# Row gathers of a graph layer with a routed feed-forward: issued in two runs, or paced by GpSimd copies

## The chip, the core and the metric

The kernel runs on one core of a Trainium2 chip. The core has a matrix engine (TensorE, PE in the profile, with its weight loads as PEld), a vector engine (VectorE, DVE), an activation engine (ScalarE, ACT), a general engine (GpSimd, POOL) and a queue engine that only issues transfers (SyncE, SP). Each engine works through its own list of instructions in order and waits on semaphores where it needs another engine's result. Transfers between the main memory and the on-chip buffers are moved by 16 DMA engines. The metric is the time of one execution on the device in microseconds (us). Three plain executions of the kernel before took 451.36 to 452.05 us, with a median of 451.93 us.

## The reference, cut to what matters

`x` has 6250 rows of 256 numbers (nodes), `src` and `dst` name the two ends of 100000 edges. The first layer is a graph attention, of which only the first 6250 edges are used:

```python
xt = jnp.matmul(x, weight).reshape(-1, heads, out_ch)       # x is layer-normed
row, col = (edge_index[0], edge_index[1])                   # src, dst
alpha_l = einsum('ehd,hd->eh', xt[row], attn_l)
alpha_r = einsum('ehd,hd->eh', xt[col], attn_r)
alpha = softmax(leaky_relu(alpha_l + alpha_r, 0.01), axis=1)
tmp = einsum('nh,nhd->nd', alpha[:n], xt[col[:n]])
out = broadcast_to(tmp[:, None, :], (n, heads, out_ch))
```

The second layer is a mixture of 8 experts with the two best of each row. A router multiplies each normed row with 8 vectors, the two largest probabilities are kept and scaled to one, and the row gets the weighted sum of two feed-forward results:

```python
logits = tokens @ router_w.T
rw, re = top_k(softmax(logits), 2); rw = rw / rw.sum(-1)
for e in range(8):
    y = gelu(tokens @ w1[e] + b1[e]) @ w2[e] + b2[e]
    out = out + combine[:, e:e+1] * y
```

Both layers add their input to their result.

## The kernel before, in words

The 6250 rows are cut into 49 tiles of 128 (`NT`), each row of a tile on one partition. The tiles form five groups, `GROUPS`, of 9, 12, 12, 9 and 7. The order of the work on each engine is the order in which the program names it; nothing is moved by a planner.

**Loads.** SP loads `x` in pieces of four tiles into one buffer for each group (`xs`), then a broadcast of the source indices (`highs` to `high_1`, L348 and L349). The row `x[dst]` that a tile needs is fetched by GpSimd: `gather(t)` (L232) is one indirect transfer of 128 rows of 1 KB. The 49 gathers land in a buffer of 9 tiles (`xd_own`) and in one of 31 tiles (`big`); tiles 40 to 48 use the places of tiles 0 to 8 again, so their gathers wait until those tiles are used up. The experts' second weights and biases are later loaded into `big` too.

**Own terms.** The first loop runs over 13 blocks of up to four tiles (`OWN`). For each block, `turn` transposes the tiles of `x` on PE (L243) and ACT copies them out (L247). `own_terms(k)` multiplies them with 12 columns on PE (L417), and ACT copies the result to the buffer `own_T` (L421), of which there are two, kept under the tag `pxs`. `back(k)` turns that result back (L430), one block later. Beside it DVE takes the statistics of the rows (`source_statistics`), and small jobs named in `fillers` are put behind blocks 1, 2, 7 and 8. The last pass of the loop turns the first block of gathered rows.

**Features.** The second loop runs over the 49 tiles in blocks of up to four. `features(g, i, ...)` multiplies the turned gathered tile with 293 columns on PE (L463), ACT copies the result to `pxs` (L471) and takes the sum of squares of the gathered row (L473, written to `junk`). `look_up` finds the attention term of the source row by matrix products (L492, L496) that DVE reduces (L500). Behind the last tile of a group, `feature_root(g)` computes the reciprocal root on GpSimd (L454 and L455). The attention and routing of group g are worked during group g+1, spread over its tiles by `tasks`: `attend_1` (from L507 on DVE), `exponents` (L521 on ACT), `attend_2`, `attend_3` (L539, L544, L545) and `route`, which ends with the write of the group's rows to a table (L588 on SP).

**After the loops.** The last group's attention and routing run alone; the rows are sorted by their pair of experts, the table's rows are gathered in that order (L897 on GpSimd), and 125 units of two matrix products each (L1073 and L1089) run the experts.

**The gathers' order.** GpSimd first makes one small copy, `last_x` (L634), that reads a late piece of `x`; so no gather starts before that piece has landed. Then come 37 gathers without anything between them. The other 12 come in `last_gathers`, which is called behind `feature_root(0)`, that is after tile 8 of the second loop; behind `feature_root(1)` `counting` makes two index tables with GpSimd (L702, L706).

Of the kernel before, what the change touches and what calls it, by code (L numbers as in the profile page):

```python
# [9 lines left out]
FP = mybir.dt.float32  # L10
# [12 lines left out]
def kernel(  # L23
# [36 lines left out]
    nc = tc.nc  # L60
# [3 lines left out]
    P = 128  # L64
    NT = -(-N // P)
    LAST = N - (NT - 1) * P
    GROUPS = [(0, 9), (9, 12), (21, 12), (33, 9), (42, 7)]
# [37 lines left out]
    held = early.enter_context(tc.tile_pool(name="held", bufs=1))  # L105
# [26 lines left out]
    xs = [held.tile([P, n, R], FP, name=f"x{g}") for g, (_, n) in enumerate(GROUPS)]  # L132
# [29 lines left out]
    def xd(t):  # L162
        k, of = (t - NOWN, big) if NOWN <= t < NOWN + BIG else (t % (NOWN + BIG), xd_own)
        return of[:, k * D : (k + 1) * D]
# [8 lines left out]
    def tiny(name, n, bufs=2):  # L173
        return small.tile([P, n], FP, name=name, bufs=bufs, tag=name)
# [33 lines left out]
    for of, pattern, k in ((count_up, [[1, 128]], 0), (number, [[0, 1]], 1)):  # L208
        nc.gpsimd.iota(
            of, pattern=pattern, base=0, channel_multiplier=k,  # L210
# [20 lines left out]
    def gather(t):  # L231
        nc.gpsimd.indirect_dma_start(  # L232
            out=xd(t), out_offset=None, in_=x[:, :],
            in_offset=bass.IndirectOffsetOnAxis(ap=dst_sb[:, t : t + 1], axis=0),
        )

    def turn(of, t0, n):

        blocks = []
        for c in range(DC):  # L240
            pt = ps.tile([128, n * P], FP, name="pt", tag="t")
            for i in range(n):
                nc.tensor.transpose(  # L243
                    pt[:, i * P : (i + 1) * P], of(t0 + i)[:, c * 128 : (c + 1) * 128], ident
                )
            tT = work.tile([128, n * P], FP, name="tT", bufs=4)
            nc.scalar.copy(tT, pt)  # L247
            blocks.append(tT)
        return blocks
# [3 lines left out]
    OWN = [  # L253
        (q, t0 + k, min(4, n - k)) for q, (t0, n) in enumerate(PARTS) for k in range(0, n, 4)
    ]
# [152 lines left out]
    rstds, own_Ts, pas = {}, {}, {}  # L408
    def source_statistics(q):
        t0, n = PARTS[q]  # L410
        rstds[q] = statistics(x_of, t0, n)

    def own_terms(k, blocks):
        n = OWN[k][2]
        pa = ps.tile([H + NE, n * P], FP, name="pa1", tag="m")
        for c in range(DC):
            nc.tensor.matmul(  # L417
                pa, own[:, c, :], blocks[c], start=(c == 0), stop=(c == DC - 1)
            )
        own_T = work.tile([H + NE, n * P], FP, name="own_T", tag="pxs")  # L420
        nc.scalar.copy(own_T, pa)  # L421
        own_Ts[k] = own_T

    def back(k):
        q, t0, n = OWN[k]
        if t0 == PARTS[q][0]:
            pas[q] = ps.tile([P, PARTS[q][1], H + NE], FP, name="pa2", tag="r")
        own_T = own_Ts.pop(k)
        for i in range(n):
            nc.tensor.transpose(  # L430
                pas[q][:, t0 - PARTS[q][0] + i, :], own_T[:, i * P : (i + 1) * P],
                ident[: H + NE, : H + NE],
            )

    def source_end(q):
        t0, n = PARTS[q]
        std = tiny("std", n)
        nc.scalar.activation(std, rstds.pop(q)[:, :, 1], AF.Sqrt, bias=eps_c)
        rstd = tiny("rstd", n)
        nc.vector.reciprocal(rstd, std)  # L440
        pa, at = pas.pop(q), slice(t0, t0 + n)
        rest = small.tile([P, H, n], FP, name="al_f")
        nc.vector.tensor_tensor(
            rest.rearrange("p h t -> p t h"), pa[:, :, :H], wide(rstd, H), ALU.mult
        )
        for k in range(3):
            nc.vector.tensor_copy(al_sb[:, k, :, at], rest)
            if k < 2:
                nc.vector.tensor_tensor(rest, rest, al_sb[:, k, :, at], ALU.subtract)
        nc.vector.tensor_copy(own_r[:, at, :], pa[:, :, H:])  # L450
# [6 lines left out]
    pxss, sqs, rstd_ds = {}, {}, {}  # L457

    def features(g, i, blocks, k):

        px = ps.tile([P, C], FP, name="px", tag="px")
        for c in range(DC):
            nc.tensor.matmul(  # L463
                px, blocks[c][:, k * P : (k + 1) * P], w_sb[:, c, :],
                start=(c == 0), stop=(c == DC - 1),
            )
        if i == 0:
            pxss[g] = work.tile([P, GROUPS[g][1], C], FP, name="pxs")
            sqs[g] = tiny("sq", GROUPS[g][1], 3)
        pxs = pxss[g]  # L470
        nc.scalar.copy(pxs[:, i, :], px)  # L471
        junk = work.tile([P, D], FP, name="junk", bufs=1)
        nc.scalar.activation(  # L473
            junk, xd(GROUPS[g][0] + i), AF.Square, bias=pxs[:, i, MEAN:],
            accum_out=sqs[g][:, i : i + 1],
        )

    def feature_root(g):
        rstd_ds[g] = tiny("rstd_d", GROUPS[g][1], 3)
        root(rstd_ds[g], sqs.pop(g), 1.0 / D)  # L480
# [149 lines left out]

    last_x = held.tile([P, 1], FP, name="last_x")
    nc.gpsimd.tensor_copy(last_x, xs[3][:, 7, :1])  # L634
    FIRST = 37
    for t in range(FIRST):
        gather(t)
    fillers = {
        1: weights_columns,
        2: pair_tables,  # L640
# [11 lines left out]
    def turn_features(k):  # L652
        g, b, n = FEATURES[k]
        return turn(xd, GROUPS[g][0] + b, n)

    source_statistics(0)
    for k, (q, t0, n) in enumerate(OWN):
        after = turn(x_of, *OWN[k + 1][1:]) if k + 1 < len(OWN) else turn_features(0)
        own_terms(k, blocks)
        blocks = after  # L660
        if k > 0:
            back(k - 1)
        if k == 0 or OWN[k - 1][0] != q:
            if q > 0:
                source_end(q - 1)
            if q + 1 < len(PARTS):
                source_statistics(q + 1)
        if k in fillers:
            fillers[k]()
# [23 lines left out]
    CUT = 26  # L693
    steps_b = mid.tile([P, TS, CUT], BF, name="steps_b", bufs=1)
    count_b = mid.tile([P, NTE], BF, name="count_b", bufs=1)
    def last_gathers():

        for t in range(FIRST, NT):
            gather(t)

    def counting():
        nc.gpsimd.iota(  # L702
            steps_b, pattern=[[1, TS], [0, CUT]], base=0, channel_multiplier=0,
            allow_small_or_imprecise_dtypes=True,
        )
        nc.gpsimd.iota(  # L706
            count_b, pattern=[[1, NTE]], base=0, channel_multiplier=0,
            allow_small_or_imprecise_dtypes=True,
        )
# [4 lines left out]
    def settle():  # L714
        while pending:
            pending.pop(0)()

    def tasks(g):

        n = GROUPS[g][1]  # L720
        at = {i: [] for i in range(n)}

        def put(i, what):
            at[min(i, n - 1)].append(what)

        if g >= 1:
            f = g - 1
            m = GROUPS[f][1]
            put(1, lambda: attend_1(f))
            put(2, lambda: exponents(f))  # L730
            put(2, lambda: attend_2(f))
            for i in range(0, m, 3):
                put(3 + i // 3, lambda i=i: attend_3(f, i, min(3, m - i)))
            steps = route(f)
            for i in range(5):
                put(7 + i // 2, lambda: next(steps))
        if g >= 2:
            f2 = g - 2
            put(1, lambda: rank(f2))
            put(2, lambda: ranked(f2))  # L740
        if g == 3:
            put(0, load_experts)
        if g == 4:
            put(0, load_biases)
        return at

    at = {}
    for k, (g, b, n) in enumerate(FEATURES):
        if b == 0:
            at = tasks(g)  # L750
        after = None
        for j in range(n):
            i = b + j
            features(g, i, blocks, j)
            if j == 0 and k + 1 < len(FEATURES):
                after = turn_features(k + 1)
            settle()
            if i % 2:
                pending.append(look_up(g, i - 1, 2))
            elif i == GROUPS[g][1] - 1:  # L760
                pending.append(look_up(g, i, 1))
            if i == GROUPS[g][1] - 1:
                feature_root(g)
                if g < 2:
                    (last_gathers, counting)[g]()
            for what in at[i]:
                what()
        blocks = after
# [4 lines left out]
    n = GROUPS[z][1]  # L773
# [73 lines left out]
    for t0, t1 in ((0, CUT), (CUT, NTE)):  # L847
        at, n = slice(t0, t1), t1 - t0
# [266 lines left out]
    for u in range(NU + LAG):  # L1115
# [17 lines left out]
        k, step = divmod(u, 4)  # L1133
# [46 lines left out]
```

## Time and profile before

The profile is of one execution that was recorded instruction by instruction. It has its own time, which differs from that of the plain executions:

| what | value |
|---|---|
| median of three plain executions | 451.93 us (451.36 to 452.05) |
| the recorded execution | 496.15 us |
| its span, first to last instruction | 494.4 us |
| mean granted clock of TensorE | 0.896 |
| PE busy | 391.3 us (79%) |
| DVE busy | 311.3 us (63%) |
| ACT busy | 227.7 us (46%) |
| POOL busy | 197.3 us (40%) |
| gathers of rows, L232 | 49, of 0.94 us each in the median, 23.7 to 129.3 us |
| expert stage, first L1073 to the end | about 250 to 494 us |

The page of a profile gives each engine's busy time, a strip of the span in 40 slices of 12.4 us, the chain of work that ended last, and the costliest groups of instructions. Behind the page, one can ask for the busy time of each engine in chosen stretches, for the instructions of one engine in order of time with what they waited for, and for the chain in order of time. An idle time whose releaser is "issue" is one in which the engine waited for nothing that the profile shows; "remote" and "another core or an unknown queue" name a releaser that is not among this core's recorded instructions.

### The profile page before, as it was taken

The page shows a single profiled execution, that of the slowest core. Times are in us where ns is not written, and L with a number is a line of the kernel's source. Part 1 is how long each engine was busy: PE and PEld are TensorE (multiplying, and loading weights), DVE is VectorE, ACT ScalarE, POOL GpSimd, SP SyncE. Part 2 cuts the span into 40 slices and gives each one's busy share as a digit, 9 for nine tenths or more (in the row PEclk, how much of TensorE's full clock was granted, in tenths as well). Part 3 has the DMA queues.
Part 4 walks back from the last instruction along what each step waited for, and adds up shares of the span by engine and source line. Part 5 has one row for each costly group of instructions (what it writes and reads, how often), then busy time and mean ns, then how long its engine had stood idle before and what let it go on. Part 6 is the DMA issues. An engine that isn't in the chain of part 4 may idle for free.

```text
span 494.4 us, 9535 instructions
## 1 busy us (share of the span) xinstructions
PE 391.3 (79%) x2442; PEld 321.8 (65%) x2442; DVE 311.3 (63%) x1051; ACT 227.7 (46%) x656; POOL 197.3 (40%) x241
## 2 busy tenths in 40 slices
PE   6970308998999971035699999999999999999992
PEld 4430003576787751024579999888988888999991
DVE  4911327425567879884368788777877687655562
ACT  2440004576676652000456675657565656633330
POOL 0177750008452101002553544676666563423232
PEclk9996557999899996555699999999999999999997
DMA  7989540003503864302666666767666676566631
GB/s 239 306 190 128 115 92 1 1 0 77 181 0 117 222 194 173 111 0 65 195 180 195 187 179 186 217 204 216 207 202 204 194 204 186 177 195 183 193 92 30
DMA packets 59091, 74.61 MB, mean 151 GB/s; under 512 B 7154, under 2 KB 54086, under 8 KB 58784
## 3 DMA queue, kind: packets, MB, share of 16 engines
q1 hardware_dynamic: 51488, 52.45, 35.1%
q0 software_dynamic: 7248, 21.29, 16.7%
q8 instruction: 22, 0.36, 0.3%
q10 hardware_dynamic: 304, 0.27, 0.2%
q14 instruction: 29, 0.24, 0.2%
HBM read 59.13 MB, written 14.87 MB: 150 GB/s over the span
## 4 chain that ended last, share of the span: by engine, by line
PE 64%; DVE 13%; issue 10%; ACT 6%; POOL 2%; another core or an unknown queue 2%; ACTq 1%; DMA 1%; POOLq 0%
PE ph L1073 21%; PE py L1089 18%; PE px L463 6%; PE pa L417 4%; PE pt L243 4%; DVE pxs L539 3%; PE pt L1019 2%; PE pi L862 2%; DVE pxs L544 2%; PE pl L492 1%; POOL xr L897 1%; ACT hid L1080 1%; DVE x L545 1%; ACT tok L986 1%
## 5 line engine op out<-in xcount | busy, mean ns | idle before, releaser
L1073 PEld LDWEIGHTS ph<-tokT,w 128*128 128x128 f32 x1000 | 131.1, 194 | 21.3 <-ACT tokT L1020 13.1
L1073 PE MATMUL ph<-tokT,w 128*128 (+1 forms) x1000 | 136.3, 280 | 7.1 <-ACT tokT L1020 6.5
L1089 PE MATMUL py<-big,hid 128*128 x500 | 129.5, 382 | 0.1
L1080 ACT ACTIVATE hid<-ph,b_cols 128x128 f32<-128x128 f32 x250 | 78.3, 366 | 99.2 <-PE ph L1073 70.0
L1089 PEld LDWEIGHTS py<-big,hid 128*128 128x128 f32 x500 | 86.0, 192 | 7.3 <-DVE acc L1096 0.4
L1096 DVE SCALAR_TENSOR_TENSOR acc<-py,shares,acc 128x256 f32 (+1 forms) x125 | 60.5, 484 | 37.9 <-PE py L1089 15.7
L1100 POOL DMA_INDIRECT out_dram<-acc,held_by x49 | 53.0, 1081 | 74.8 <-DVE acc L1096 60.6
L897 POOL DMA_INDIRECT xr<-table,held_by x49 | 49.5, 1010 | 56.4 <-DVE held_by L884 40.0
L1096 DVE SCALAR_TENSOR_TENSOR acc<-big,shares,acc (+1 forms) x125 | 60.7, 486 | 8.9 <-issue 4.9
L463 PE MATMUL px<-w_sb,tT 128*128 128x293 f32 x196 | 56.8, 422 | 3.1 <-ACT pxs L471 2.7
L986 ACT ACTIVATE tok<-xr,nm 128x256 f32<-128x256 f32 x49 | 29.7, 605 | 46.9 <-DVE xr L993 39.0
L247 ACT COPY tT<-pt 128x512 f32<-128x512 f32 (+2 forms) x54 | 27.2, 541 | 42.5 <-issue 18.5
L463 PEld LDWEIGHTS px<-w_sb,tT 128*128 128x128 f32 x196 | 34.8, 193 | 10.9 <-ACT pxs L471 3.2
L243 PE MATMUL pt<-ident,x 128*128 128x128 f32 x98 | 17.5, 329 | 28.1 <-ACT tT L247 21.5
L454 POOL TENSOR_SCALAR sq<-sq 128x9 f32<-128x9 f32 (+2 forms) x5 | 1.2, 245 | 83.8 <-ACT junk L473 70.6
L232 POOL DMA_INDIRECT big<-in_x_dram,dst_sb x31 | 29.4, 949 | 10.2 <-issue 9.2
L243 PEld LDWEIGHTS pt<-ident,x 128*128 128x128 f32 x98 | 13.3, 168 | 30.8 <-ACT tT L247 21.9
L471 ACT COPY pxs<-px 128x293 f32<-128x293 f32 x49 | 19.7, 403 | 25.5 <-PE px L463 21.3
L1008 ACT ACTIVATE acc<-xr,nm 128x256 f32<-128x256 f32 x49 | 29.2, 598 | 0.0
L417 PE MATMUL pa<-tT,own 128*12 128x512 f32 (+1 forms) x52 | 26.5, 637 | 0.0
L1019 PE MATMUL pt<-ident,tok 128*128 128x128 f32 x98 | 19.3, 280 | 7.8 <-ACT tok L986 7.8
L500 DVE TENSOR_REDUCE ag<-pl 128x8 f32<-128x392 f32 (+1 forms) x26 | 13.9, 538 | 14.9 <-PE pl L496 14.9
(206 smaller groups left out, 484.9 us busy)
## 6 DMA issues: line engine op xcount, KB each, us to landing
w<-in_L_ffn_w_dram SPq DMA_DIRECT2D x125, 256.0 KB
x<-in_x_dram SPq DMA_DIRECT2D x11, 512.0 KB
table<-x SPq DMA_DIRECT2D x2, 2022.0 KB
table<-x SPq DMA_DIRECT2D x2, 1516.5 KB
big<-in_L_ffn_w_dram SPq DMA_DIRECT2D x2, 1024.0 KB
high<-highs SPq DMA_DIRECT2D x1, 1568.0 KB
table<-x SPq DMA_DIRECT2D x1, 1179.5 KB
big<-in_L_ffn_b_dram SPq DMA_DIRECT2D x1, 1024.0 KB
```

What stands on the lines that cost most here:

```text
L232: nc.gpsimd.indirect_dma_start(out=xd(t), out_offset=None, in_=x[:, :], in_offset=bass.IndirectOffsetOnAxis(ap=dst_sb[:, t : t + 1], axis=0),)
L243: nc.tensor.transpose(pt[:, i * P : (i + 1) * P], of(t0 + i)[:, c * 128 : (c + 1) * 128], ident)
L417: nc.tensor.matmul(pa, own[:, c, :], blocks[c], start=(c == 0), stop=(c == DC - 1))
L463: nc.tensor.matmul(px, blocks[c][:, k * P : (k + 1) * P], w_sb[:, c, :], start=(c == 0), stop=(c == DC - 1),)
L897: nc.gpsimd.indirect_dma_start(out=xr[:, i, :], out_offset=None, in_=table[:, :], in_offset=bass.IndirectOffsetOnAxis(ap=held_by[:, s0 + i ...
L986: nc.scalar.activation(tok[:, i, :], xr[:, i, :D], AF.Identity, bias=bias[:, i : i + 1], scale=scale[:, i : i + 1],)
L1008: nc.scalar.activation(acc[:, s * D : (s + 1) * D], xr[:, i, :D], AF.Identity, bias=bias[:, i : i + 1], scale=more[:, i : i + 1],)
L1073: nc.tensor.matmul(ph[:, j, :], w[:, c * F + j * 128 : c * F + (j + 1) * 128], tokT[:, bass.ds(rows_at + c * TS, TS)], start=(c == 0), sto ...
L1080: nc.scalar.activation(hid[:, j, :], ph[:, j, :], AF.Gelu, bias=b1_cols[:, :, j][:, bass.ds(at_act[u][0], 1)])
L1089: nc.tensor.matmul(py, hid[:, j, :], we2[:, j, bass.ds(at_pe[u][1], D)], start=(j == 0), stop=(j == FC - 1),)
L1096: nc.vector.scalar_tensor_tensor(to, y, share, to, op0=ALU.mult, op1=ALU.add)
L1100: nc.gpsimd.indirect_dma_start(out=ends_at[s][:, :], out_offset=bass.IndirectOffsetOnAxis(ap=held_by[:n, s : s + 1], axis=0), in_=acc[:n, ...
```

## The change

The copy `last_x` and the run of 37 gathers behind it are taken out, and so is `last_gathers` with its 12. A helper, `paced(t, n, of)`, makes one small GpSimd copy that reads `of`, so that GpSimd waits until `of` is written, and then issues the gathers of tiles t to t+n-1. It is called in two places. In the loop over own terms it comes behind each of the last ten blocks (k = 3 to 12), reads that block's `own_T` (12 partitions, one element each) and issues two gathers, 20 in all. In the loop over features it comes behind each tile's `features`, reads one column of that tile's `pxs` (128 partitions, one element each) and issues the gather of the tile 20 further on; this happens for tiles 0 to 28, 29 gathers. `counting` stays behind `feature_root(1)`.

```diff
-    last_x = held.tile([P, 1], FP, name="last_x")
-    nc.gpsimd.tensor_copy(last_x, xs[3][:, 7, :1])
-    FIRST = 37
-    for t in range(FIRST):
-        gather(t)
+    AHEAD = 20
+    OWN_FROM = len(OWN) - AHEAD // 2
+    pace = held.tile([P, 1], FP, name="pace")
+
+    def paced(t, n, of):
+
+        nc.gpsimd.tensor_copy(pace[: of.shape[0]], of)
+        for i in range(t, min(t + n, NT)):
+            gather(i)
+
...
         own_terms(k, blocks)
+        if k >= OWN_FROM:
+            paced(2 * (k - OWN_FROM), 2, own_Ts[k][:, :1])
         blocks = after
...
-    def last_gathers():
-
-        for t in range(FIRST, NT):
-            gather(t)
-
...
             features(g, i, blocks, j)
+            if GROUPS[g][0] + i + AHEAD < NT:
+                paced(GROUPS[g][0] + i + AHEAD, 1, pxss[g][:, i, :1])
...
                 feature_root(g)
-                if g < 2:
-                    (last_gathers, counting)[g]()
+                if g == 1:
+                    counting()
```

## The prediction

> **What bounds the kernel now.** I read the page's strip first and found a hole in an otherwise busy PE row at about 36 to 76 us. Then I asked for the busy times by stretch there. Columns: stretch, its length, busy us (and instructions) of PE, PEld, DVE, ACT, POOL, then the granted clock, the DMA share and GB/s.
>
> ```profile
> 24.00:36.00 12.00, 10.02 (x49) 4.38 (x48) 1.37 (x55) 5.00 (x9) 9.26 (x10) 1.00 0.81 191
> 36.00:48.00 12.00, 0.41 (x4) 0.32 (x4) 1.36 (x13) 0.67 (x2) 8.41 (x10) 0.66 0.94 115
> 48.00:60.00 12.00, 4.95 (x12) 1.83 (x12) 1.94 (x10) 0.96 (x2) 8.96 (x11) 0.50 0.53 126
> 60.00:72.00 12.00, 1.24 (x5) 0.50 (x4) 4.91 (x15) 0.57 (x1) 8.22 (x9) 0.64 0.48 104
> 72.00:84.00 12.00, 7.47 (x27) 3.44 (x28) 7.19 (x35) 4.55 (x9) 0.00 (x0) 0.63 0.03 6
> 84.00:96.00 12.00, 11.94 (x65) 5.64 (x63) 6.50 (x21) 6.45 (x15) 0.00 (x0) 1.00 0.00 1
> ```
>
> For 36 us PE and ACT nearly stand still while POOL issues gathers (0.94 us each, one per 1.25 us). ACT's list in order of time says who holds whom:
>
> ```profile
> 35.89 0.57 ACT L421 COPY own_T<-pa 12x512 f32<-12x512 f32 x1 [2.97 <-PE pa L417]
> 47.79 0.58 ACT L247 COPY tT<-pt 128x512 f32<-128x512 f32 x1 [11.33 <-issue]
> 55.52 0.58 ACT L247 COPY tT<-pt 128x512 f32<-128x512 f32 x1 [7.14 <-issue]
> 66.72 0.57 ACT L421 COPY own_T<-pa 12x512 f32<-12x512 f32 x1 [10.61 <-issue]
> 75.89 1.08 ACT L247 COPY tT<-pt 128x512 f32<-128x512 f32 x2 [8.60 <-remote]
> ```
>
> ACT starts four copies 7 to 11 us late, and no recorded instruction is what it waits for; PE waits for ACT. It ends when the gathers have landed. The chain in order of time gives the size:
>
> ```profile
> 33.63 2.18 PE pa L417 x4
> ...
> 78.50 3.00 PE pa L417 x4
> ...
> 82.87 1.82 PE pa L417 x4
> ...
> 86.05 1.82 PE pa L417 x4
> ...
> 117.22 1.01 PE px L463 x4
> ...
> 127.45 1.66 PE px L463 x4
> ```
>
> Undisturbed, own-term blocks follow each other by 86.05 - 82.87 = 3.18 us. From 33.63 to 78.50 lie two blocks: 44.87 - 6.36 = **38.5 us stalled**. A smaller stall lies under the last 12 gathers: the four tiles from 117.22 take 10.2 us, the four before (from 110.73) 6.5 and the four behind (to 134.34) 6.9, so about **3.5 us**. Together 42.0 us.
>
> **Which of this is in the time asked for?** The recorded execution took 496.15 us, the plain ones 451.93: 44.2 more. I looked for where recording could cost so much. From 250 to 480 us PE is busy 225 of 230 us at clock 1.00: nothing to give back. In the features stage the engines run closely packed outside the two stalls; from 190 to 228 us DVE is busy 30.5 of 38. The only holes of this size are the stalls, and 494.4 - 42.0 = 452.4, plus the 1.75 us around the span, is 454.1, still 2.2 above the median. So the plain runs have the stalls' cost hardly at all. Here the Trainium skill (Runtime: NRT & Kernel Launch, "The ~15µs preamble/postamble breakdown") says otherwise: a profile's total is about 6.2 us above the plain execution, whatever the kernel. By that, only 6.2 of the 44.2 would be recording; some 38 us would still have no place, and a stall taken for real would make the changed kernel 451.93 - 42.0 = 409.9. The row of two measured times decides: a PE-bound stage of 230 us cannot hide 38 us. I count the stalls as belonging to the recorded execution.
>
> **The change, part by part.**
>
> *First run of gathers removed, own-term pacing added.* Ten GpSimd copies, each like `last_x` (0.24 us, then 0.19 us to the next start), and two gathers each: 0.43 + 1.25 + 1.15 = 2.8 us on POOL per block, below the 3.18 us of a block, so POOL keeps up. The copy adds a reader to `own_T`, of which there are two: ACT's copy of block k+2 now waits for POOL's of block k. That is 6.4 us of room; if POOL lost its lead wholly it would cost the excess, block by block. Rows 0 to 3 are asked for at blocks 3 and 4 and turned behind block 11, over 20 us later. In the recorded run the stall should go, up to 38.5 us; in the plain runs I put this at 0. Bounds for plain: a gain up to about 3 us (if other recording costs of 5 us exist, 5 - 2.2 = 2.8 of the stall is real), a loss of 0.5. What is late next once the stall goes is PE itself, whose transposes and products fill 3.18 us a block.
>
> *`last_x` removed.* Its wait until 23.3 us held gathers from the loads of `x`; the new first gather follows the `own_T` of block 3 (ACT, 27.5 us), later still. The broadcast for `high_1` is issued at 26.4 us and needed behind block 8, at 15.0 + 8 x 3.2 = 41 us undisturbed. It now competes with about 12 gathers instead of 14 by then. Zero.
>
> *Last 12 gathers moved, one per tile for tiles 0 to 28.* Each tile: 0.24 + 0.19 + 1.08 (a gather behind another operation, 112.62 us) + about 0.05 = 1.56 us on POOL, against a tile time of 6.4/4 = 1.6 us on PE in group 0 and 1.7 to 2.0 later. A gather leads its use by 20 tiles, minus up to 8 for the turning ahead: 12 x 1.6 = 19 us, against some 4 us from the last issue of the first run (69.7 us) to the quiet queue. No PE wait for data. All are issued by tile 28, before the experts' load at tile 33, and the table writes on SP wait for DVE, not for POOL; a gather that meets a table write has those same 19 us to spare.
>
> *Behind the waiting copies in POOL's queue* stand the roots of groups 0 and 1 and the two tables. DVE waits for the roots already:
>
> ```profile
> 134.82 0.21 POOL L454 TENSOR_SCALAR sq<-sq 128x12 f32<-128x12 f32 x1 [5.50 <-ACT junk L473]
> ...
> 137.45 0.21 DVE L507 TENSOR_TENSOR z<-pxs,rstd_d 128x48 f32<-128x48 f32 x1 [2.51 <-POOL rstd_d L455]
> ...
> 140.64 0.23 ACT L521 ACTIVATE ex<-lr 128x48 f32<-128x48 f32 x1
> ```
>
> Tile 20's copy can start when its `pxs` is there (134.10), so the root starts at 134.10 + 0.24 + 0.19 + 1.08 + 0.05 = 135.66, **0.84 us later**. DVE's chain L507 to L515 ends at 138.63 and ACT takes its result at 140.64, so 2.0 us are covered: cost 0. For group 0 the result is ready at 113.6 and ACT takes it at 117.9: covered too. `counting` (5.2 us) is needed at 214 us.
>
> *Port.* The Trainium skill (SBUF — State Buffer, "Who interferes with whom") speaks against the change: a DVE operation with two SBUF inputs and a GpSimd operation that reads SBUF exclude each other for their whole length. The trace shows gathers under DVE's L539 and L544 lengthened from 0.95 to 1.31, 1.56 and 1.73 us (120 to 125 us), while L539 stays at 1.05 us. So here POOL pays and DVE doesn't. By the row, a tile under attention costs POOL 0.43 + 1.53 + 0.05 = 2.0 us, equal to the tile time, no lag. By the rule, each copy may first wait a whole L539, 3.2 us at worst with the longest gather: 1.2 us lag per tile, over tiles 12 to 14 some 3.6 us; or DVE waits for copies, at most 29 x 0.24 = 7 us, of which only the 8 tiles in group 2, where DVE nears its limit, can count (2 us). No row has such a copy beside L539, so I keep -0.2 to +2 as bounds and take 0, by the gathers' rows.
>
> Sum for the plain time: 0 + 0 + 0 + 0 = no change, **451.9 us**. For the recorded execution: 496.15 - 42.0 = about 454 us.
>
> **Rivals.**
>
> 1. *A part of the stall is real (faster).* For it: the stall is the one thing that the change attacks, and it is large. Against it: the sum above leaves no room unless recording costs something elsewhere. With 3 to 5 us of such cost, 0.8 to 2.8 us of stall are real; middle 1.8, time **450.1**.
> 2. *POOL falls behind (slower).* Place: tiles 12 to 14, DVE's attention of group 0, by the port rule. With 3.6 us of lag, less 0.16 a tile over six tiles (1.72 - 1.56), 2.6 us are left at tile 20, plus 0.84: the root is 3.4 us late against 2.0 covered. ACT then waits 1.4 us in front of L521, in a stage where PE is full, and DVE's attention of group 1 moves too: **453.3**. It decides as soon as the root of group 1 starts over 2.0 us behind its last L473.
> 3. *Pacing does not end the stall.* Gathers still come at 2 per 3.18 us = 0.63 per us, against 0.80 in the run before; the expert stage has 98 indirect transfers in some 250 us, 0.39 per us, without such holes. The recorded execution may keep a part; the plain time would be 451.9 as in the forecast.
>
> **Chances.** A measurement of this kernel can tell 0.2% (0.9 us) from no change. Forecast, with rival 3 inside it: 0.40 (rival 3 is 0.10 of it). Rival 1: 0.31. Rival 2 and other delays at POOL: 0.29. The forecast's own range is 451.0 to 452.8. With the bounds of the unknown costs (-3 and +2.3, with a few tenths of run-to-run spread) the range is 448.6 to 454.4.
>
> **What would show it.** ACT's 7 to 11 us waits by "issue" at L247 and L421 gone, own-term blocks 3.2 us apart throughout, the recorded time near 454: the first step. The recorded time falling by 40 us while the plain one stays: the reading of the stalls. POOL's wait in front of L454 by "ACT junk" gone at group 1 and L507's idle near 3.3 us: the covered delay. If the plain time falls by more than 3 us, the accounting is wrong and the stall was real; if it rises by more than 1 us, L521's wait for DVE or a wait of ACT for POOL at L421 or L471 will show it.

## The result, and the profile after

The changed kernel takes 454.33 us in the median of six executions (453.47 to 456.1), against 451.48 us (450.12 to 452.05) for the kernel before on the same chip: a ratio of 1.0068 with an interval of 1.0044 to 1.0093. It is **slower by some 3 us**, where no change was forecast. The recorded execution, one of the six, took 454.36 us.

The page's strip of the changed kernel (slices of 11.3 us), with PE and POOL:

```profile
span 452.6 us, 9611 instructions
...
PE   6999999988966104559999999999998999999991
...
POOL 0036888999411000245534366676665654233222
```

Busy times by stretch of the changed kernel, in the columns of the prediction's first table:

```profile
36.00:48.00 12.00, 12.00 (x63) 5.67 (x61) 10.21 (x46) 6.27 (x14) 8.77 (x10) 1.00 0.77 77
48.00:60.00 12.00, 11.94 (x67) 7.16 (x66) 5.65 (x18) 6.93 (x19) 10.05 (x13) 1.00 0.52 82
60.00:72.00 12.00, 11.61 (x76) 9.26 (x75) 2.06 (x4) 8.90 (x29) 10.48 (x18) 1.00 0.54 102
```

The hole from 36 to 76 us is gone; PE is full there. But the kernel before, recorded a second time (`before_again`), has no hole either:

```profile
span 449.4 us, 9535 instructions
...
PE   5999999998965105468999999999998999999991
...
POOL 0076878772011000345444366666674754233222
```

The same gathers and the same recording are in both, and none of the 66 plain executions of the kernel before on record took over 452.77 us. So the hole in the first record was a disturbance of that one execution, and the change did not remove it. The comparison that counts is with undisturbed records.

**Where the time went.** Count from the first L463 of a tile to that of a later one. Tiles 8 to 20 take 20.03 us in `before_again` and in after alike, and the own-term blocks 3 to 12 take 28.00 us in both. Tiles 20 to 38 take 31.83 us in `before_again` and 34.41 in after. What ends late there is shown by POOL's list around the root of group 1 (its last tile, 20, starts at 86.92 us), in order of time, of the changed kernel:

```profile
78.20 0.94 POOL L640 COPY pace<-pxs 128x1 f32<-128x1 f32 x1
79.30 1.29 POOL L232 DMA_INDIRECT big<-in_x_dram,dst_sb  x1 [0.16 <-issue]
80.60 1.04 POOL L640 COPY pace<-pxs 128x1 f32<-128x1 f32 x1
81.81 1.29 POOL L232 DMA_INDIRECT big<-in_x_dram,dst_sb  x1 [0.16 <-ACT junk L473]
83.11 0.58 POOL L640 COPY pace<-pxs 128x1 f32<-128x1 f32 x1
...
93.62 0.97 POOL L232 DMA_INDIRECT xd_own<-in_x_dram,dst_sb  x1 [0.16 <-issue]
94.67 0.21 POOL L454 TENSOR_SCALAR sq<-sq 128x12 f32<-128x12 f32 x1
```

No copy here waits for another engine's tile (the gaps of 0.16 us stand in front of gathers): POOL is itself behind, and works copy and gather back to back until the root. The root could start 2.32 us behind the start of tile 20, when that tile's L473 is done (the first record before has it so). It starts at 94.67 - 86.92 = 7.75 us, that is **5.43 us late**. The same root in `before_again`:

```profile
89.63 0.96 POOL L232 DMA_INDIRECT xd_own<-in_x_dram,dst_sb  x1 [0.30 <-issue]
90.66 0.21 POOL L454 TENSOR_SCALAR sq<-sq 128x12 f32<-128x12 f32 x1
```

There it is 5.2 us behind tile 20, 2.87 late: in undisturbed records the last 12 gathers of the kernel before stand in front of this root too, which the first record did not show. From the root the delay runs to DVE, to ACT and to PE. DVE, ACT and PE of the changed kernel, from their lists in order of time:

```profile
97.31 0.21 DVE L507 TENSOR_TENSOR z<-pxs,rstd_d 128x48 f32<-128x48 f32 x1 [7.22 <-POOL rstd_d L455]
```

```profile
98.52 0.24 ACT L521 ACTIVATE ex<-lr 128x48 f32<-128x48 f32 x1 [3.37 <-DVE lr L515]
```

```profile
99.10 1.26 PE L463 MATMUL px<-w_sb,tT 128*128 128x293 f32 x4 [1.47 <-ACT pxs L471]
...
107.75 0.41 PE L492 MATMUL pl<-al_sb,high 128*128 128x196 bf16 x3 [0.82 <-DVE ag L500]
...
112.00 0.41 PE L492 MATMUL pl<-al_sb,high 128*128 128x196 bf16 x3 [1.41 <-DVE ag L500]
```

ACT stands 3.37 us in front of L521 because its input is late; the copies of `px` (L471) stand behind it, and PE waits for those. In `before_again` the same L521 waits 0.79 us:

```profile
94.49 0.24 ACT L521 ACTIVATE ex<-lr 128x48 f32<-128x48 f32 x1 [0.79 <-DVE lr L515]
```

### The profile page after: what moved, and what is told of

Its sections match the earlier page's. It is cut to its first block, busy times and chain, and to the rows that moved or that the text cites. A ratio compares the mean times of both kernels' runs of the same rounds, so it can differ in the third digit from the quotient of the medians.

```text
span 452.6 us, 9611 instructions
## 1 busy us (share of the span) xinstructions
PE 386.4 (85%) x2442; PEld 321.3 (71%) x2442; DVE 310.6 (69%) x1051; ACT 229.7 (51%) x656; POOL 213.1 (47%) x279
## 4 chain that ended last, share of the span: by engine, by line
PE 48%; DVE 21%; issue 12%; POOL 10%; DVEq 2%; DMA 2%; ACT 2%; POOLq 1%; ACTq 0%; SPq 0%
PE ph L1078 15%; PE py L1094 14%; DVE acc L1101 8%; PE pa L417 5%; PE px L463 5%; PE pt L243 4%; DVE pxs L539 2%; DVE stats L975 2%; POOL xr L902 2%; DVEq L1038 2%; POOL nm L981 2%; POOL out_dram L1105 2%; DVE pxs L544 1%; POOL xd_own L232 1%; DMA table<-x 1%
## 5 line engine op out<-in xcount | busy, mean ns | idle before, releaser
L1078 PEld LDWEIGHTS ph<-tokT,w 128*128 128x128 f32 x1000 | 132.8, 196 | 17.2 <-ACT tokT L1025 11.4
L463 PE MATMUL px<-w_sb,tT 128*128 128x293 f32 x196 | 55.7, 416 | 1.9 <-ACT pxs L471 1.5
L463 PEld LDWEIGHTS px<-w_sb,tT 128*128 128x128 f32 x196 | 34.2, 190 | 9.6 <-ACT pxs L471 2.0
L232 POOL DMA_INDIRECT big<-in_x_dram,dst_sb x31 | 34.8, 1121 | 6.1 <-issue 4.2
L471 ACT COPY pxs<-px 128x293 f32<-128x293 f32 x49 | 19.7, 403 | 24.4 <-PE px L463 19.4
L417 PE MATMUL pa<-tT,own 128*12 128x512 f32 (+1 forms) x52 | 24.1, 588 | 0.0
L492 PE MATMUL pl<-al_sb,high 128*128 128x196 bf16 x147 | 18.6, 246 | 4.8 <-DVE ag L500 4.8
L965 DVE TENSOR_TENSOR xr<-xr 128x512 f32<-128x512 f32 (+1 forms) x25 | 17.0, 680 | 6.2 <-DMA xr<-table,held_by 4.6
L492 PEld LDWEIGHTS <-high 128*128 128x128 bf16 x147 | 13.4, 97 | 11.0 <-issue 7.4
L980 POOL TENSOR_SCALAR mv<-mv 128x2 f32<-128x2 f32 (+1 forms) x25 | 5.7, 229 | 32.5 <-DVE mv L977 29.3
```

The source lines that it names most:

```text
L232: nc.gpsimd.indirect_dma_start(out=xd(t), out_offset=None, in_=x[:, :], in_offset=bass.IndirectOffsetOnAxis(ap=dst_sb[:, t : t + 1], axis=0),)
L417: nc.tensor.matmul(pa, own[:, c, :], blocks[c], start=(c == 0), stop=(c == DC - 1))
L463: nc.tensor.matmul(px, blocks[c][:, k * P : (k + 1) * P], w_sb[:, c, :], start=(c == 0), stop=(c == DC - 1),)
L492: nc.tensor.matmul(pl[:, k, :, :], high_1[:, t * P : (t + 1) * P], al_sb[:, part, :, :], start=(part == 0), stop=False,)
L1078: nc.tensor.matmul(ph[:, j, :], w[:, c * F + j * 128 : c * F + (j + 1) * 128], tokT[:, bass.ds(rows_at + c * TS, TS)], start=(c == 0), sto ...
```

## The experiments

Ratios are to the kernel before on the same chip, with 95% intervals. "Late" is how far group 1's root starts above its floor of 2.32 us behind tile 20.

| kernel | median us | ratio | late us | tiles 20 to 38, us |
|---|---|---|---|---|
| before_again, before_third (records) | 451.14, 451.4 | | 2.87, 2.87 | 31.83, 31.84 |
| after | 454.33 | 1.0068 (1.0044 to 1.0093) | 5.43 | 34.41 |
| counting_later | 454.41 | 1.0086 (1.0071 to 1.0102) | 5.40 | 34.47 |
| before_late_root | 458.32 | 1.0164 (1.0151 to 1.0178) | 5.90 | 34.87 |
| root_first | 457.07 | 1.0128 (1.0111 to 1.0146) | 0 | 36.05 |
| early_own | 452.85 | 1.0047 (1.0034 to 1.0061) | 2.75 | 31.73 |
| burst20 | 453.12 | 1.0046 (1.0025 to 1.0066) | 2.74 | 31.72 |
| no_copies | 450.85 | 1.0000 (0.9989 to 1.0012) | 1.61 | 30.92 |
| early_no_copies | 451.0 | 1.0001 (0.9988 to 1.0015) | 0 | 30.90 |

### Is the hole real? before_again

The kernel before, unchanged, recorded once more.

> The kernel before, unchanged, recorded once more. If the 42 us hole of its first record is what recording does to a burst of gathers, it is there again and the recorded execution takes over 490 us. If it was a disturbance of that one execution (the kernel before_late_root has the same burst and its record has no hole), the record takes about 451 us, and the interval from tile 20's features to tile 38's is 30.9 us as in the first record.

Measured: 451.14 us, no hole, PE full from 24 to 96 us. The first record's 496.15 us is one disturbed execution.

### Does a late root cost what it seems to? before_late_root

The kernel before, in which `counting` (5.2 us of POOL) is put ahead of group 1's root, behind a small copy of the last tile's `pxs`:

```diff
             if i == GROUPS[g][1] - 1:
+                if g == 1:
+                    nc.gpsimd.tensor_copy(last_x, pxss[g][:, i, :1])
+                    counting()
                 feature_root(g)
-                if g < 2:
-                    (last_gathers, counting)[g]()
+                if g == 0:
+                    last_gathers()
```

> The kernel before with one thing added to the wait: the two index tables (5.4 us) are held by a copy of tile 20's features and stand in front of the root of group 1 instead of behind it. All gathers are as before. Theory A: the root starts about 4.9 us later, 2.0 are covered, the time rises by 2.5 to 3.3 us over the kernel before. Theory B: only the order of work off the path is changed, no loss beyond 0.5 us.

POOL in order of time, of this kernel:

```profile
90.58 5.26 POOL L702 IOTA steps_b<- 128x3328 bf16 x1
...
96.06 0.21 POOL L454 TENSOR_SCALAR sq<-sq 128x12 f32<-128x12 f32 x1
```

With no change in how gathers are paced, a root 5.90 us late stretches tiles 20 to 38 to 34.87 us, 3.0 us above `before_again`. L521 waits 3.8 us for DVE. So the late root alone makes after's pattern. The plain time rose by more than the 2.5 to 3.3 us expected: 1.64% of 451 = 7.4 us. Of the rest, the record shows some 2 us in the expert stage (246.3 us against about 244, from the first product of L1073 to the last; the first stands at 237.8 us in the first record, not at about 250) and 2.4 us in front of tile 0, of which more below; why the expert stage is longer stays open.

### Does the root's place repair it? root_first

The changed kernel, with the copies and gathers of group 1's last six tiles (tiles 15 to 20) moved behind group 1's root:

```diff
-                paced(GROUPS[g][0] + i + AHEAD, 1, pxss[g][:, i, :1])
+                if g == 1 and i >= 6:
+                    behind.append((GROUPS[g][0] + i + AHEAD, 1, pxss[g][:, i, :1]))
+                else:
+                    paced(GROUPS[g][0] + i + AHEAD, 1, pxss[g][:, i, :1])
...
                 feature_root(g)
                 if g == 1:
+                    for held_back in behind:
+                        paced(*held_back)
                     counting()
```

> The changed kernel with the paced gathers of tiles 15 to 20 put behind the root of group 1 in GpSimd's queue; the same copies and gathers, another order. Theory A (GpSimd is behind, the root of group 1 starts 5.4 us later than in the kernel before, of which 2.0 are covered, and that is the loss): the root starts about 1 us or less after its last square sum, vector's wait for it falls from 7.2 to under 3 us, and the time returns to that of the kernel before, 451.5 (+0.3 to -0.3%). Theory B (the copies and the spread gathers cost the vector and activation engines time wherever the root stands): no gain, 454.3. Theory C (the loss comes from the 5.25 us index table in front of the gathers and the root of group 2): no gain, 454.3.

POOL and then DVE in order of time:

```profile
89.46 0.21 POOL L454 TENSOR_SCALAR sq<-sq 128x12 f32<-128x12 f32 x1 [2.75 <-ACT junk L473]
...
118.78 0.20 POOL L454 TENSOR_SCALAR sq<-sq 128x12 f32<-128x12 f32 x1
```

```profile
121.40 0.21 DVE L507 TENSOR_TENSOR z<-pxs,rstd_d 128x48 f32<-128x48 f32 x1 [9.55 <-POOL rstd_d L455]
```

Group 1's root is on time, but the six gathers and `counting` now stand in front of group 2's root, which is 9.84 us late; PE loses there instead, and the kernel is slower than after, which none of the three theories had expected. The work held back was moved, not hidden, so this time neither confirms theory A nor refutes it.

### Is it counting in front of group 2's root? counting_later

After, with `if g == 2: counting()` in place of `if g == 1`.

> The changed kernel with the two index tables moved from behind the root of group 1 to behind the root of group 2. Theory C: the root of group 2 starts 5 us earlier and up to 3 us come back, 451.5 to 452.5. Theory A: that root's delay was covered, time unchanged at 454.3 (within 0.4).

Group 2's root comes back to 2.32 us behind its tile, from 6.14 in after; the time does not move (454.41). A delay of 3.8 us at group 2 is covered; `counting` has no part in the loss. One more suspect falls with it: in after, ACT waits 2.27 us for POOL's copy in front of the L471 at 113.94 us. Here that wait is gone, with no gain.

### Which of the two pacings makes POOL late? early_own, burst20, no_copies, early_no_copies

In `early_own` the two gathers stand behind the first ten own-term blocks, not the last ten:

```diff
-    OWN_FROM = len(OWN) - AHEAD // 2
+    OWN_FROM = 0
...
-        if k >= OWN_FROM:
+        if k < AHEAD // 2:
```

> The changed kernel with the ten own-term pairs paced by blocks 0 to 9 instead of 3 to 12, so that three blocks are free of gathers before the features. Theory A, with the 4.5 us gather under the vector engine's two long table operations as the source of the lag: GpSimd is idle when the features begin, the lag at tile 20 is what the attention of group 0 leaves (about 2 us or less, covered), time 451.5 to 452.3. If the attention alone makes the lag, the root of group 1 is still over 4 us late: 454. Theory B: 454.3. The recorded execution may show more of the stall, since gathers start at 17 us.

In `burst20` the first 20 gathers are issued in one run behind a single copy, and nothing is paced in the own-term loop:

```diff
+    paced(0, AHEAD, xs[3][:, 7, :1])
...
-        if k >= OWN_FROM:
-            paced(2 * (k - OWN_FROM), 2, own_Ts[k][:, :1])
```

> The changed kernel with its first 20 gathers issued in one run behind one copy (as the kernel before starts them) and only the other 29 paced by the features. Theory A: GpSimd is free when the features begin; the lag at tile 20 is that of the attention of group 0 alone, as in early_own: the root of group 1 2.8 us late, 1.9 covered, 0.9 lost, 451.7 (451.2 to 452.3). If the pacing in the own-term loop is itself what costs, the same. If the paced copies of the features cost all of the loss, 454.

In `no_copies` the own-term pacing stays, and the other 29 gathers keep their places but lose their copies:

```diff
-                paced(GROUPS[g][0] + i + AHEAD, 1, pxss[g][:, i, :1])
+                gather(GROUPS[g][0] + i + AHEAD)
```

> The changed kernel without the 29 small copies in the features loop; the gathers stay behind the same tiles in GpSimd's queue, but nothing holds them. Theory A: GpSimd needs 1.25 us a tile instead of 1.34 to 2.4 and doesn't wait for the vector engine's tensor operations; the root of group 1 is about 2.1 us late, nearly covered: 450.9 to 451.8. If the gathers' place behind the tiles is what costs, 454.

`early_no_copies` has the edits of `early_own` and of `no_copies`.

> Both repairs together: two gathers behind each of the first ten own-term blocks, and no copies in front of the 29 later gathers. If the lateness of group 1's root is the whole cause, it should fall to its floor of about 2.3 us behind tile 20 (no_copies 3.93, early_own 5.07), the stretch from tile 20 to 38 to 30.9 us, and the plain time to that of no_copies, 450 to 451 us: a root that is less than 1.9 us late costs nothing already, so there is nothing more to win. If the gathers' later start costs time by itself, this version gains on no_copies, to 449 to 450 us. If early issue costs (more transfers beside the loads of x), it is slower, 452 us as early_own.

The four versions make a square: with the 29 copies 1.0068 and 1.0047 (own-term pacing late, early), without them 1.0000 and 1.0001. **The copies in front of the 29 gathers are the loss.** That the late own-term pacing adds to it where the copies are there is shown by the records (the root is 5.43 us late against 2.75); in the plain times the intervals of the two overlap. Two expectations were missed: `early_own` and `burst20` came out at 452.85 and 453.12 us, both above 452.3, the top of what their lag at the root was expected to cost. From `no_copies` to after, tiles 20 to 38 grow by 34.41 - 30.92 = 3.49 us, and the plain ratios differ by 0.0068, that is 3.1 us.

The own-term loop gives POOL its first lag. POOL of after, in order of time, and DVE beside it:

```profile
44.42 0.18 POOL L640 COPY pace<-own_T 12x1 f32<-12x1 f32 x1 [0.27 <-ACT own_T L421]
45.10 4.50 POOL L232 DMA_INDIRECT big<-in_x_dram,dst_sb  x1 [0.50 <-issue]
49.91 0.95 POOL L232 DMA_INDIRECT big<-in_x_dram,dst_sb  x1 [0.30 <-issue]
50.87 0.18 POOL L640 COPY pace<-own_T 12x1 f32<-12x1 f32 x1
```

```profile
45.10 2.62 DVE L647 TENSOR_TENSOR low<-count_up,low 128x2401 bf16<-128x2401 f32 x1
47.64 1.84 DVE L650 TENSOR_SCALAR high<-high,number 128x6272 bf16<-128x6272 bf16 x1
```

One gather takes 4.50 us in place of 0.95. It ends at 49.60, 0.12 us behind DVE's L650 (49.48), the second of two long table operations (fillers 7 and 8). The second began only at 47.64; a gather of 0.95 us would have been done at 46.05, so it was held under the first one already. In `before_again` a gather that began at 44.71, inside the first of them, ends 0.12 us behind the second too, and in each of the eleven later records one gather ends 0.12 to 0.13 us behind it. That DVE holds it is read from these ends; no run took the two operations away. From then on the copies name no releaser: their tile is always ready. Tile 0's copy runs at 61.18 us, 6.2 us behind the start of its tile; in `burst20`, where POOL had stood idle, it runs 1.9 us behind it.

Then POOL catches up slowly: copy, gap and gather follow each other by 1.34 us a tile (0.20 + 0.16 + 0.98), against 1.49 on PE in group 0 and 1.67 in group 1. Behind tile 8 the root of group 0 takes 2.1 us of POOL, and under the attention of group 0 it loses again. In after the three tiles from 78.20 cost POOL 2.40, 2.51 and about 2.0 us. Each of the three copies ends 0.03 to 0.05 us behind an L539 of DVE (79.14, 81.64 and 83.69 against 79.10, 81.61 and 83.64):

```profile
78.04 1.06 DVE L539 TENSOR_TENSOR pxs<-pxs,alpha 128x864 f32<-128x864 f32 x1
...
80.56 1.05 DVE L539 TENSOR_TENSOR pxs<-pxs,alpha 128x864 f32<-128x864 f32 x1
...
82.59 1.05 DVE L539 TENSOR_TENSOR pxs<-pxs,alpha 128x864 f32<-128x864 f32 x1
```

Without copies (`early_no_copies`, POOL in order of time) the gathers there are the ones that the prediction had read, and a wait for ACT is back in front of the root:

```profile
79.67 1.31 POOL L232 DMA_INDIRECT big<-in_x_dram,dst_sb  x1 [0.30 <-DMA big<-in_x_dram,dst_sb]
81.29 1.56 POOL L232 DMA_INDIRECT big<-in_x_dram,dst_sb  x1 [0.30 <-issue]
83.15 1.73 POOL L232 DMA_INDIRECT big<-in_x_dram,dst_sb  x1 [0.30 <-issue]
...
89.65 0.21 POOL L454 TENSOR_SCALAR sq<-sq 128x12 f32<-128x12 f32 x1 [0.99 <-ACT junk L473]
```

**The cover.** Of all these roots, lateness less the time lost in tiles 20 to 38 (over 30.85 us, that stretch in the first record, whose root was on time) is nearly one number: 2.87 - 0.98, 5.43 - 3.56, 5.40 - 3.62, 5.90 - 4.02, 2.75 - 0.88, 1.61 - 0.07: 1.5 to 1.9 us. That is the slack at L521, put at 2.0 in the prediction.

### What the records do not account for: before_third, early_own_again

`early_own` and the kernel before lose the same at the root, yet their plain times differ by 2.1 us; and `no_copies`, which loses less, is not faster than before. The kernel before and `early_own` were recorded again.

> The kernel before, recorded once more, to see how late its root of group 1 usually is. If single records are typical, the root starts about 2.9 us above its floor as in before_again (5.2 us behind tile 20) and tiles 20 to 38 take 31.8 us. If before_again was late by chance, which is what the plain times of no_copies and early_no_copies (no gain from a root at its floor) speak for, the root starts less than 2 us above the floor and the stretch takes 30.9 to 31.0 us.

> early_own recorded once more. Its plain time is 2.1 us above before, its record lost only 0.9 us at the root of group 1. If that record was typical, the stretch from tile 20 to 38 is 31.7 us again, and about 1.2 us of its plain loss lie elsewhere; if it was a good one, the root is 4 us or more above its floor and the stretch takes 33 us.

Both records repeat: the root is 2.87 and 2.76 us late, and the stretch takes 31.84 and 31.73 us. The whole records, cut at the starts of tile 0 and of tile 48:

| record | tile 0 starts, us | tiles 0 to 48, us | behind, us | span, us |
|---|---|---|---|---|
| before_again | 53.52 | 85.77 | 310.09 | 449.38 |
| before_third | 53.67 | 85.99 | 309.98 | 449.64 |
| after | 54.98 | 86.94 | 310.68 | 452.60 |
| early_own | 53.83 | 85.83 | 310.65 | 450.31 |
| early_own_again | 55.31 | 85.92 | 310.48 | 451.71 |
| no_copies | 56.19 | 83.44 | 310.46 | 450.09 |
| early_no_copies | 55.39 | 83.44 | 310.45 | 449.28 |

Two things differ beside the root.

*The clock at tiles 42 to 48.* Of the 2.4 us between the kernel before and the two versions without copies in tiles 0 to 48, 0.9 is the root and 1.5 lies in tiles 42 to 48, where TensorE's clock drops for a moment. A table by stretch shows it, first `early_own`, then `no_copies`:

```profile
130.00:136.00 6.00, 4.60 (x23) 3.38 (x22) 2.99 (x13) 0.46 (x2) 0.00 (x0) 0.72 0.72 247
```

```profile
119.00:140.00 21.00, 17.38 (x116) 13.82 (x115) 18.12 (x46) 12.59 (x40) 2.18 (x2) 1.00 0.75 195
```

The drop is in the undisturbed records of before, of `early_own` and `burst20` and of `before_late_root`; in those of after, `counting_later` and the two without copies tiles 42 to 48 run at full clock, and `root_first` has it earlier, at tile 38. What comes in front of it is a lull of PE, and that is in all records. The next rows are cut at the edges of the clock's slots, which are 3.41 us long; first `before_again`, then after:

```profile
127.50:130.91 3.41, 1.35 (x11) 0.83 (x10) 3.10 (x13) 2.16 (x7) 0.00 (x0) 1.00 0.00 0
130.91:134.33 3.42, 3.00 (x16) 2.31 (x16) 2.00 (x8) 0.00 (x0) 0.00 (x0) 0.50 0.81 290
```

```profile
129.29:132.70 3.41, 2.77 (x16) 2.01 (x15) 3.13 (x10) 1.69 (x6) 1.03 (x1) 1.00 0.37 115
132.70:136.11 3.41, 1.57 (x15) 1.27 (x15) 3.13 (x13) 0.97 (x4) 0.00 (x0) 1.00 0.14 49
```

In `before_again` most of the lull lies in one slot (PE busy for 1.35 us of it), and the next slot runs at half clock; in after it is spread over two, and the clock stays. From tile 0 to tile 48 all twelve records agree: PE was busy for 1.53 us or less in the slot in front of every half-clock slot, for 1.57 or more in front of every other. So these 1.5 us seem to hang on where the lull falls in the slots, and not on the gathers as such; no run moved the one without the other.

*The start.* Tile 0 starts up to 1.5 us apart in two records of one kernel. They differ already at about 10 us, in front of all gathers, in eight weight loads of PE that take 192 ns in `early_own` and 333 in `early_own_again`:

```profile
L324 PEld LDWEIGHTS pa<-terms,turned x8: 187/192/193, 9.8 to 10.6; 128*128 128x128 f32 x8
```

```profile
L324 PEld LDWEIGHTS pa<-terms,turned x8: 321/333/333, 9.8 to 11.3; 128*128 128x128 f32 x8
```

The fast kind is in `before_again`, `before_third`, `counting_later` and `early_own`, and their first L417 starts at 13.4 to 13.8 us; in the other eight, the first record of the kernel before among them, it starts at 14.7 to 15.3. So the start is one of the execution, not of the kernel alone.

*What is left.* From `before_again` to after the span grows by 3.22 us: 1.46 in front of tile 0, 2.58 in tiles 20 to 38, 1.41 less in tiles 42 to 48, 0.59 behind tile 48. Only the 2.58 are traced to the change. With `no_copies` as the base, root and clock give +3.5 for after and +2.4 for `early_own` in tiles 0 to 48; their plain times are 3.1 and 2.1 above. By the same stretch the kernel before should be 2.4 us above `no_copies`, and the plain times are equal. The whole records are nearly equal too, since its two records start tile 0 by 1.7 to 2.7 us earlier. How often the plain executions of each kernel have the fast start and the half-clock slot is not on record, so this part **stays open**, and single records do not settle 2 us.

## Why the prediction was wrong

- **The stall in the record, and which of it is in the plain time.** That the plain time would gain nothing from its end was right. The reason was wrong: the hole belonged to one execution, not to the recording. `before_again` has no hole, so the changed record shows nothing that the change cured. That the recorded time of about 454 us came out at 454.36 is luck: own-term blocks 3 to 12 and tiles 8 to 20 took 69.34 and 24.55 us in the first record against 28.00 and 20.03 undisturbed, 45.9 us and not 42.0, and the late root put some 3 us back. The 6.2 us by the rule that was set aside (the Trainium skill, Runtime: NRT & Kernel Launch, "The ~15µs preamble/postamble breakdown") do not show either: the later records lie within about 1.5 us of the plain times. Whether the two times that the page compares are those compared here, no run shows.
- **Own-term pacing, "POOL keeps up".** The sum of 2.8 us per block against 3.18 holds for all paced blocks but one. There two DVE operations hold a gather for 4.50 us and the lag stays. In the record that I read, these two began at 84.6 us, behind the stall, when POOL issued nothing; the disturbed record hid the collision. `own_T`'s buffers cost PE nothing, as put.
- **`last_x` removed: zero.** Nothing in the records speaks against it.
- **The last 12 gathers in new places, 1.56 us per tile.** Outside the attention of group 0 it was 1.34, faster than put. No PE wait for data appeared; the root, not the data, was late.
- **"The root starts ... 0.84 us later", "covered: cost 0". This is the step that failed.** The cover was sized well (1.9 us against 2.0). The lateness was not: 5.43 us in place of 0.84, so 3.56 us were left uncovered in place of 0. The working let tile 20's copy start when its `pxs` was there, which takes POOL to be waiting. POOL was not waiting but had a lag from two places: what was left of the 4.3 us of the own-term loop, 2.7 (after less `early_own`), and 2.75 from the root of group 0 and the copies and gathers beside its attention (`early_own` alone). The disturbed record had a part in this as well: in it group 1's root waits 5.50 us for ACT, while in the undisturbed ones the kernel before has a late root itself, which costs 0.98 of the 3.56 us.
- **Port: "I ... take 0, by the gathers' rows".** The taken 2.0 us a tile was too low and the rule's 3.2 too high: 2.40, 2.51 and 2.0. The copies took 0.94, 1.04 and 0.58 us in place of 0.2 and ended with an L539 of 1.05 us, as the rule of the Trainium skill (SBUF — State Buffer, "Who interferes with whom") has it: whoever comes second waits until the other's instruction is over. The gathers beside them were shorter (1.29) than in the row that I used, so wait and lengthening are not simply added. DVE did not pay: L539 stays at 1.05 us.
- **Rival 2** named the mechanism and the place, with L521's wait as its sign, and 453.3 us. Its lag was 3.4 us in place of 5.43, for lack of the own-term part. Rival 1 fell with the hole. Rival 3 had nothing to act on: no later record has the stall, with or without pacing, and what caused it is unknown.

## What to carry to other kernels

A wait put in front of cheap issues on an in-order queue is paid by what stands behind them: ask for the queue's backlog at the next instruction that another engine needs, and do not start that sum from an empty queue. Look for the longest operations of DVE that fall into the stretch; two of them made a lag of 4.3 us, of which 2.7 was left twenty tiles later. And before a large hole in one record is explained, record the kernel a second time, and add up whole records, not only the stretch in which a change is expected.

## What the hardware showed that I had not expected

- A gather's issue on GpSimd can be held for the length of two DVE operations in a row: 3.4 to 4.5 us in place of 0.95, in all eleven later records, with its end 0.12 to 0.13 us behind DVE's second.
- One execution can stand for some 40 us in the middle of a kernel, with no releaser in the trace that would say why; none of the eleven later records did.
- TensorE's granted clock falls to half for 3.41 us inside a stage that else runs at 1.00, behind a slot of 3.41 us in which PE was busy for at most 1.53 us, and it stays where the same lull is spread over two slots (2.77 and 1.57 us in after). It costs 1.5 us at tiles 42 to 48.
- The weight loads of PE at about 10 us take 192 ns in four records and 333 in eight. The two records of `early_own` are one of each kind, and their tile 0 starts 1.5 us apart.
